# Gated attention with a routed expert layer: turned rows read back two tiles later, the router bias added once, left sums and gathers first in the attention's first step

## The chip, the cores and the metric

One core of a Trainium2 chip runs the whole program. The metric is the device time of one execution in microseconds (us). A profile is one execution recorded by the hardware profiler; its span runs from the first to the last instruction of the program. TensorE is called PE in the profile (its weight loads PEld), VectorE DVE, ScalarE ACT, GpSimd POOL and SyncE SP.

## The reference

The input x has two sequences of 1024 tokens with 512 features, in 32-bit floats.

```python
xn = layernorm(x)
# attention, one head of width 512
qkv = einsum('bsh,oh->bso', xn, w_qkv) + b_qkv
q, k, v = split(qkv, 3)
s = softmax(q @ k.T / sqrt(512)) @ v @ w_out.T + b_out
# expert layer: 8 experts, top 2
logits = xn @ router_w + router_b
topk_vals, topk_idx = top_k(logits, 2)
w = softmax(topk_vals)
h = silu(xn @ expert_w[e] + expert_b[e])      # for each expert e
combined = sum of w * h over a token's two experts
y = xn + combined @ proj_w + proj_b
g = silu(norm_w * y / sqrt(mean(y * y) + 1e-6))
out = x + s * g
```

## The kernel before, in words

The 2048 tokens are 16 tiles of 128 rows. Every engine runs its instructions in the order in which the program writes them down; semaphores keep them apart where one needs another's result. Almost all transfers are issued by SP on one queue; the stores of the experts' results (`ho_d`) are issued by ACT, the gathers by POOL. A tile of 128 x 512 floats is 256 KB.

**The loop over the tiles** (24 to 91 us). The weights of values and output are multiplied beforehand into `rwvo`, which also holds the router's columns. For tile t, `value_side(t)` multiplies the turned rows `xnT` by `rwvo` into two PSUM banks `pv` (the big pool has two such pairs, so `pv` of tile t needs what tile t - 2 held); `keep_values(t)` copies 512 columns to `vo` (ACT, L461) and the nine columns of the router and of the bias's product to `lg` (DVE, L462). In the text pv6 is the product of tile 6, vo6 and lg6 its copies.

The rows have to be normalised and turned first. `stats(g)` takes mean and variance of tiles 2g and 2g + 1 (DVE), and a square root (ACT, `std`); `shifts(g)` makes their reciprocal and shift (DVE); `rows(g)` writes the normalised rows `xn` (ACT, L333) and then issues on SP, in this order: for the tiles from 4 on a put of the rows to a scratch `xn_s` in HBM (four blocks of 128 x 128), the loads of x for tiles 8 later, the stores of the rows to `xn_d`, which the gathers read later, and again from tile 4 on the reads `xz` of the scratch (`take`). `turn_x(t)` then turns `xz` by a DVE transpose of 32 x 32 blocks (L120); tiles 0 to 3 (`DIRECT`) are turned by PE and copied by DVE (L378). Buffers: 8 of x, 5 of xn, 6 of xz, 6 of the scratch. `norm(g)` is the three together. Before the loop stand `rows(0)` and `norm(2)`; in the loop

```python
        if t == 1:
            rows(1)
            norm(3)
        if t == 3:
            turn_x(4)
            turn_x(5)
        if t % 2 == 0 and 0 < t and t + 6 < NT:
            norm(t // 2 + 3)
```

and for t from 4 on `turn_x(t + 2)` ahead of `value_side(t)`. At t = 4 SP issues four loads of the key weights `wZ`, which DVE turns at t = 8 (`turn_w`), at t = 9 and 10 DVE makes two weighted sums (`sk`, `vb`), which PE needs at t = 11 and 12.

**Routing, queries and experts** (91 to 256 us). DVE picks each token's two experts from `lg` and sorts the tokens by expert in 39 slots of 128, while PE makes the product of the query and key weights and the queries of the first sequence. Then each slot's rows are gathered (POOL), turned by way of a scratch (SP, DVE), multiplied (PE, L771), biased (DVE, L797), passed through silu (ACT, L800) and stored to `ho_d` (ACT's queue, L801).

**Attention and the rest** (256 to 541 us). Pairs of tiles go through a product of 2 x 2 blocks with seven multiplications instead of eight (Strassen's, in Winograd's form), which needs sums of blocks: `sum_left(k)` of the queries (POOL, `sw`), `sum_right` of the keys (DVE, `tw`), `sum_values` of the values (DVE, `tv`), `sum_p` of the probabilities (POOL). `scores(t)` makes the scores of tiles 0 and 1 in the plain way; `pair_scores(k)` those of a later pair, and `softmax` puts the probabilities to a scratch, which `take_p` reads back and `turn_p` turns. `fetch(t)` gathers a token's two experts' results (POOL), `scale_c` (ACT) and `combine` (DVE) add them with their weights and put them to a scratch, `take_c` and `turn_c` turn them, `project` multiplies them by `proj_w` (PE). `fetch_x` loads the rows for the sum with `proj_b`, which `add_b` makes (POOL). `queries_of(k)` makes queries of the second sequence (PE, ACT L538). `attend(k)` multiplies probabilities by values. The first step is written out at the end of the kernel, ahead of `for k in range(NP)`. Its buffers come from pool `at`, whose places are dealt out in the order in which tiles are first opened, over the room that the experts' pool `mo` has left.

Of the kernel before, what the change touches and what calls it, by code (L numbers as in the profile page):

```python
# [27 lines left out]
def kernel(  # L28
# [45 lines left out]
    def close(guard):  # L74
        guard.__exit__(None, None, None)
# [38 lines left out]
    def take(z, d):  # L114

        sp.dma_start(z.rearrange("p i f -> p (i f)"), d.rearrange("q (a i) f -> (q a) (i f)", i=4))
# [224 lines left out]
    def rows(g):  # L341

        two = (2 * g, 2 * g + 1)
        for t in two:
            xn_[t] = ln.tile([P, H], FP, tag="xn", name=f"xn{t}", bufs=5)
            normed(in_turn(xn_[t]), own(x[t]), t)
        if two[0] >= DIRECT:
            for t in two:
                xs[t] = dram.tile([4, P, P], FP, tag="xn_s", name=f"xn_s{t}", bufs=6)
                put(xs[t], xn_[t])  # L350
        for t in two:
            if t + 8 < NT:
                load_x(t + 8)
        for t in two:
            sp.dma_start(xn_d[ts(t, P), :], xn_[t])
        if two[0] >= DIRECT:
            for t in two:
                xz[t] = ln.tile([P, 4, P], FP, tag="xz", name=f"xz{t}", bufs=6)
                take(xz[t], xs.pop(t))

    def norm(g):
        stats(g)
        shifts(g)
        rows(g)
# [3 lines left out]
    def turn_x(t):  # L368
        dst = xnT[t // ST][:, :, ts(t % ST, P)]
        if t >= DIRECT:  # L370
            turn(dst, xz.pop(t))
            return
        ps = ps_mm.tile([P, 512], FP, tag="mm", name=f"xt{t}").rearrange(
            "p (j f) -> p j f", j=KC
        )
        for j in range(KC):
            pe.transpose(ps[:, j, :], xw[t][:, ts(j, P)], ident)
        dve.tensor_copy(dst, ps)  # L378
# [79 lines left out]
    def keep_values(t):  # L458
        pv = pvs.pop(t)
        dst = vo[t // ST][:, t % ST, :].rearrange("p (n f) -> p n f", n=2)  # L460
        act.copy(dst, pv[:, :, 0:HH])  # L461
        dve.tensor_tensor(lg1[:, t, :], pv[:, 0, HH : HH + E1], rb, ALU.add)  # L462


    for t in range(NT):
        if 3 < t < NT - 2:
            turn_x(t + 2)
        value_side(t)
        if t:
            keep_values(t - 1)  # L470
        if t == 1:
            rows(1)
            norm(3)
        if t == 3:
            turn_x(4)
            turn_x(5)
        if t % 2 == 0 and 0 < t and t + 6 < NT:
            norm(t // 2 + 3)
        if t == 2:
            gps.dma_start(bo, b_out.partition_broadcast(P))  # L480
        if t == 4:
            spread(sp, wZ[1], w_qkvT[:, ts(1, H)])
        if t == 8:
            turn_w(wqkT[:, KC:], wZ[1])
        if t == 9:
            sk_ = weighted(wqkT[:, KC:], bqk[:, 0], "sk")
        if t == 10:

            vb = weighted(wo, bqkv[:, 2], "vb")
        if t == 11:  # L490
            dve.tensor_copy(u, columns(sk_, "pu"))
        if t == 12:
            pvb = ps_mm.tile([P, 512], FP, tag="mm", name="pvb")
            pe.matmul(pvb, lhsT=ones, rhs=vb, start=True, stop=True)
            dve.tensor_tensor(bo, pvb, bo, ALU.add)
            close(raw_guard)
            ew_guard, ewp = pool("ew", side="right")
            ew = ewp.tile([P, E, KC, H], FP, name="ew")
            for e in range(E):
                sp.dma_start(ew[:, e], expert_w[e].rearrange("(c p) f -> p c f", p=P))  # L500
    keep_values(NT - 1)
    close(ln_guard)
    eb_guard, ebp = pool("eb", side="right")
    eb = ebp.tile([P, E, H], FP, name="eb")
# [397 lines left out]
    def sum_right(b):  # L902
        w_ = at.tile([P, 3, KH, 512], FP, tag="tw", name=f"tw{b}", bufs=1)
        return right_sums(right(b), w_, dve, 1)
# [156 lines left out]
    def take_p(t):  # L1061
        pz[t] = at.tile([P, 4, 2 * P], FP, tag="pz", name=f"pz{t}")
        take(pz[t], ps_.pop(t))
# [98 lines left out]
    def both_of(step, k, odd_first=False):  # L1162
        if k < NP:
            for t in (2 * k + 1, 2 * k) if odd_first else (2 * k, 2 * k + 1):
                step(t)


    keys, vals = sum_right(0), sum_values(0)
    for _ in range(2):
        next(keys)  # L1170
    sum_left(1)
    both_of(fetch, 0)
    sp.dma_start(pb, proj_b.partition_broadcast(P))
    both_of(fetch_x, 0)
    both_of(add_b, 0)
    sp.dma_start(nw, norm_w.partition_broadcast(P))
    scores(0)
    next(keys)
    for _ in range(3):
        next(vals)  # L1180
    take_p(0)
    scores(1)
    close(ps_guard)
    ps_guard, ps_s = pool("ps_s", bufs=4, space=PSUM)
    tw[0] = next(keys)
    both_of(scale_c, 0)
    both_of(inverse, 0)
    both_of(combine, 0)
    tv[0] = next(vals)
    take_p(1)  # L1190
    both_of(take_c, 0)
    both_of(fetch, 1)
    queries_of(0, lambda name: ps_mm.tile([P, 512], FP, tag="mm", name=name))
    for k in range(NP):
        more = k + 1 < NP
        final = k + 2 == NP
# [123 lines left out]
```

## Time and profile before

| what | us |
|---|---|
| median of 3 runs | 543.29 |
| lowest and highest | 541.87, 545.43 |
| the profiled execution's own time | 542.69 |
| its span | 541.0 |
| PE busy | 527.2 |
| DVE busy | 314.9 |
| POOL busy | 217.7 |
| ACT busy | 156.9 |

A line of a group or of the timeline names the engine, the line of the kernel, the operation and "out<-in" by the program's names, buffer numbers left out; idle time before it stands in brackets with what ended it. An instruction of PE on 32-bit floats shows as two records, so a product of four matmuls is eight records. The chain that ended last is followed back from the last instruction, at each step to what released it.

### The profile page before, as it was taken

How to read it: one execution, taken by the hardware profiler on the slowest of the kernel's cores; microseconds unless marked ns; L12 is line 12 of the kernel's file. 1: busy time of each engine (PE TensorE's matmuls, PEld its weight loads, DVE VectorE, ACT ScalarE, POOL GpSimd, SP SyncE). 2: the span in 40 equal slices, each digit the busy share in tenths (PEclk: the TensorE clock that was granted, in tenths of full speed). 3: DMA queues.
4: the chain of work that ended last, by engine and by line, in shares of the span. 5: the costliest groups of instructions: out<-in, count | busy, mean ns of one | idle time of the engine just before them, and what ended most of it. 6: DMA issues, size and time to landing. Idle time of an engine off the chain costs nothing.

```text
span 541.0 us, 5784 instructions
## 1 busy us (share of the span) xinstructions
PE 527.2 (97%) x1754; PEld 320.9 (59%) x1754; DVE 314.9 (58%) x529; ACT 156.9 (29%) x259; POOL 217.7 (40%) x231
## 2 busy tenths in 40 slices
PE   8979999999999999999999999999999999999996
PEld 6867887444444444444466666756746657484486
DVE  3645763841333333334689467376697685949595
ACT  2454312111211111111331622422425234152340
POOL 5000000023353874200276545346279755465551
PEclk9998999999999999999999999999999999999999
DMA  8879939939999999995566832723624628295502
GB/s 241 223 224 329 278 127 343 406 103 318 284 306 320 344 333 314 302 279 137 176 210 217 286 123 85 285 79 109 242 78 168 241 84 291 73 332 173 207 27 79
DMA packets 90928, 118.66 MB, mean 219 GB/s; under 512 B 6928, under 2 KB 55184, under 8 KB 90768
## 3 DMA queue, kind: packets, MB, share of 16 engines
q1 hardware_dynamic: 79344, 89.16, 51.4%
q0 software_dynamic: 5792, 18.88, 10.9%
q10 hardware_dynamic: 5760, 10.23, 5.0%
q8 instruction: 15, 0.25, 0.2%
q14 instruction: 17, 0.14, 0.1%
HBM read 73.69 MB, written 44.56 MB: 219 GB/s over the span
## 4 chain that ended last, share of the span: by engine, by line
PE 74%; DMA 10%; DVE 8%; issue 4%; ACT 1%; POOL 1%; SPq 1%; DVEq 0%; POOLq 0%; ACTq 0%
PE ph L771 20%; PE so L1104 17%; PE pp L1033 12%; PE po L970 10%; PE pq L512 5%; PE pv L450 4%; DMA wZ<-in_L_attn_w_qkv_dram 3%; PE pqk L543 3%; DMA xn_s<-xn 2%; PE pr L531 2%; DMA ho_d<-h 2%; DVE sc L1039 1%; DVE pT L120 1%; DMA xn_d<-xn 1%; DMA wo<-in_L_attn_w_out_dram 1%
## 5 line engine op out<-in xcount | busy, mean ns | idle before, releaser
L771 PE MATMUL ph<-ew,gT 128*128 x280 | 120.3, 592 | 0.0
L745 POOL DMA_INDIRECT xg<-xn_d,tok x39 | 37.2, 955 | 164.0 <-DVE npast L690 103.4
L771 PEld LDWEIGHTS ph<-ew,gT 128*128 128x128 f32 x280 | 53.2, 190 | 67.0 <-issue 67.0
L797 DVE TENSOR_TENSOR h<-ph,eb 128x512 f32<-128x512 f32 x39 | 26.9, 690 | 85.0 <-issue 53.1
L450 PE MATMUL pv<-rwvo,xnT 128*128 128x256 f32 (+1 forms) x256 | 60.3, 393 | 4.6 <-DVE lg L462 4.3
L450 PEld LDWEIGHTS pv<-rwvo,xnT 128*128 128x128 f32 x256 | 48.8, 194 | 15.0 <-DVE lg L462 6.3
L800 ACT ACTIVATE h<-h 128x512 f32<-128x512 f32 x39 | 24.6, 631 | 100.2 <-DVE h L797 97.4
L970 PE MATMUL po<-pw,ct 128*128 128x512 f32 x112 | 49.2, 592 | 0.0
L1001 ACT ACTIVATE pr<-sc,nm 128x1024 f32<-128x1024 f32 x16 | 18.3, 1146 | 89.5 <-DVE nm L998 78.4
L1111 DVE TENSOR_TENSOR o<-so,o 128x256 f32<-128x256 f32 x49 | 20.0, 421 | 39.2 <-PE so L1104 28.5
L1149 POOL TENSOR_TENSOR o<-o,base 128x512 f32<-128x512 f32 x14 | 20.6, 1491 | 47.6 <-DVE o L1114 47.6
L1033 PE MATMUL pp<-xnT,qT 128*128 128x512 f32 x84 | 39.5, 592 | 0.0
L1104 PE MATMUL so<-vo,pT 128*128 128x256 f32 x168 | 38.5, 379 | 0.0
L932 POOL DMA_INDIRECT hg<-ho_d,posi_m x32 | 32.4, 1014 | 13.2 <-issue 7.5
L970 PEld LDWEIGHTS po<-pw,ct 128*128 128x128 f32 x112 | 21.3, 190 | 25.5 <-issue 25.1
L1104 PEld LDWEIGHTS so<-vo,pT 128*128 128x128 f32 x168 | 31.9, 190 | 7.3 <-issue 2.6
L1039 DVE TENSOR_TENSOR sc<-pp,sc 128x512 f32<-128x512 f32 x49 | 31.6, 680 | 3.3 <-PE pp L1033 3.2
L120 DVE STREAM_TRANSPOSE gT<-sz 128x512 f32<-128x512 f32 x39 | 27.3, 701 | 7.1 <-DMA sz<-xs 7.1
L531 PE MATMUL pr<-xnT,wqk 128*128 128x256 f32 x128 | 29.2, 382 | 1.9 <-DVE sc L1039 1.9
L531 PEld LDWEIGHTS pr<-xnT,wqk 128*128 128x128 f32 x128 | 24.0, 190 | 8.1 <-DVE sc L1039 4.2
L120 DVE STREAM_TRANSPOSE pT<-pz 128x1024 f32<-128x1024 f32 x14 | 28.2, 2015 | 0.0
L512 PE MATMUL pq<-xnT,wqk 128*128 128x512 f32 x64 | 28.1, 594 | 0.0
(214 smaller groups left out, 773.0 us busy)
## 6 DMA issues: line engine op xcount, KB each, us to landing
xs<-xg SPq DMA_DIRECT2D x39, 256.0 KB, 4.7
sz<-xs SPq DMA_DIRECT2D x39, 256.0 KB, 4.7
ho_d<-h ACTq DMA_DIRECT2D x39, 256.0 KB, 4.9
ew<-in_L_ffn_expert_w_dram SPq DMA_DIRECT2D x8, 1024.0 KB, 13.4
ps<-pr SPq DMA_DIRECT2D x16, 512.0 KB, 2.9
pz<-ps SPq DMA_DIRECT2D x16, 512.0 KB, 4.9
x<-_attn_hidden_states_dram SPq DMA_DIRECT2D x16, 256.0 KB, 5.5
xn_d<-xn SPq DMA_DIRECT2D x16, 256.0 KB, 4.7
```

Source lines behind the costliest of these rows:

```text
L120: dve.transpose(dst.rearrange(f"p j {order} -> p i j a", a=QP), z.rearrange("p i (j b) -> p i j b", b=QP),)
L450: pe.matmul(pv[:, n, : HH + E1 * (1 - n)], lhsT=xnT[t // ST][:, c, ts(t % ST, P)], rhs=rwvo[:, c, cols], start=(c == 0), stop=(c == KC - 1),)
L512: pe.matmul(ps[:, half, :], lhsT=wqk[:, c, ts(oc, P)], rhs=xnT[0][:, c, ts(half, 512)], start=(c == 0), stop=(c == KC - 1),)
L531: pe.matmul(ps[:, :PW], lhsT=wqk[:, c, ts(oc, P)], rhs=xnT[1][:, c, ts(k, PW)], start=(c == 0), stop=(c == KC - 1),)
L745: gps.indirect_dma_start(out=xg[s], out_offset=None, in_=xn_d, in_offset=bass.IndirectOffsetOnAxis(ap=tok[:, s : s + 1], axis=0),)
L771: pe.matmul(ph, lhsT=g_[:, c, :], rhs=ew[:, ds(r, 1), c, :].rearrange("p e f -> p (e f)"), start=(c == 0), stop=(c == KC - 1),)
L797: dve.tensor_tensor(h, ph, eb[:, ds(r, 1), :].rearrange("p e f -> p (e f)"), ALU.add)
L932: gps.indirect_dma_start(out=g_, out_offset=None, in_=ho_d, in_offset=bass.IndirectOffsetOnAxis(ap=posi_m[:, n, t : t + 1], axis=0),)
L970: pe.matmul(po, lhsT=c_[:, c, :], rhs=pw[:, c, :], start=(c == 0), stop=(c == KC - 1))
L1033: pe.matmul(ps, lhsT=l_[:, c, :], rhs=r_[:, c, :], start=(c == 0), stop=(c == KH - 1))
L1039: dve.tensor_tensor(dst, ps, other, ALU.add)
L1104: pe.matmul(ps[:, :w_], lhsT=l_[:, c, :], rhs=r_[:, c, :], start=(c == 0), stop=(c == SK - 1),)
```

## The change

In the loop over the tiles, the reads of the turned rows leave `rows` and become `reads(g)`, which is called two tiles later than before or at the same tile ahead of the next `norm`; `norm(3)` moves from tile 1 to tile 2, behind `keep_values(1)`; xn has six buffers and xz five. The nine router columns are copied by ACT without a bias, and the bias `rb` is added to all 16 tiles at once after the loop. In the attention's first step `sum_left(1)` and `fetch(0)` stand first, the loads of `proj_b`, of the rows and of `norm_w` stand behind `take_p(0)`, and `inverse`, the last sum of values and `queries_of(0)` stand ahead of `scale_c` and `combine`.

```diff
@@ rows(g)
-            xn_[t] = ln.tile([P, H], FP, tag="xn", name=f"xn{t}", bufs=5)
+            xn_[t] = ln.tile([P, H], FP, tag="xn", name=f"xn{t}", bufs=6)
...
         for t in two:
             sp.dma_start(xn_d[ts(t, P), :], xn_[t])
-        if two[0] >= DIRECT:
-            for t in two:
-                xz[t] = ln.tile([P, 4, P], FP, tag="xz", name=f"xz{t}", bufs=6)
-                take(xz[t], xs.pop(t))
+    def reads(g):
+        for t in (2 * g, 2 * g + 1):
+            xz[t] = ln.tile([P, 4, P], FP, tag="xz", name=f"xz{t}", bufs=5)
+            take(xz[t], xs.pop(t))
@@ keep_values(t)
-        dve.tensor_tensor(lg1[:, t, :], pv[:, 0, HH : HH + E1], rb, ALU.add)
+        act.copy(lg1[:, t, :], pv[:, 0, HH : HH + E1])
@@ the loop over the tiles
         if t == 1:
             rows(1)
+            reads(2)
+        if t == 2:
             norm(3)
         if t == 3:
             turn_x(4)
             turn_x(5)
+            reads(3)
+        if t % 2 == 0 and 2 < t and t + 4 < NT:
+            reads(t // 2 + 2)
         if t % 2 == 0 and 0 < t and t + 6 < NT:
             norm(t // 2 + 3)
...
     keep_values(NT - 1)
+    dve.tensor_tensor(lg1, lg1, rb.unsqueeze(1).to_broadcast([P, NT, E1]), ALU.add)
@@ the attention's first step
+    sum_left(1)
+    both_of(fetch, 0)
     keys, vals = sum_right(0), sum_values(0)
     for _ in range(2):
         next(keys)
-    sum_left(1)
-    both_of(fetch, 0)
-    sp.dma_start(pb, proj_b.partition_broadcast(P))
-    both_of(fetch_x, 0)
-    both_of(add_b, 0)
-    sp.dma_start(nw, norm_w.partition_broadcast(P))
     scores(0)
     next(keys)
     for _ in range(3):
         next(vals)
     take_p(0)
+    sp.dma_start(pb, proj_b.partition_broadcast(P))
+    both_of(fetch_x, 0)
+    both_of(add_b, 0)
+    sp.dma_start(nw, norm_w.partition_broadcast(P))
     scores(1)
     close(ps_guard)
     ps_guard, ps_s = pool("ps_s", bufs=4, space=PSUM)
     tw[0] = next(keys)
+    both_of(inverse, 0)
+    tv[0] = next(vals)
+    queries_of(0, lambda name: ps_mm.tile([P, 512], FP, tag="mm", name=name))
     both_of(scale_c, 0)
-    both_of(inverse, 0)
     both_of(combine, 0)
-    tv[0] = next(vals)
     take_p(1)
     both_of(take_c, 0)
     both_of(fetch, 1)
-    queries_of(0, lambda name: ps_mm.tile([P, 512], FP, tag="mm", name=name))
```

## The prediction

> **What bounds the kernel now.** I read the page first (header, busy shares, slices), then the waits of the stretch from 24 to 95 us, the timeline of the same stretch, the table by windows, the chain of work that ended last, and the timeline from 250 to 300 us. The page:
>
> ```profile
> span 541.0 us, 5784 instructions
> PE 527.2 (97%) x1754; PEld 320.9 (59%) x1754; DVE 314.9 (58%) x529; ACT 156.9 (29%) x259; POOL 217.7 (40%) x231
> PE   8979999999999999999999999999999999999996
> DMA  8879939939999999995566832723624628295502
> ```
>
> TensorE works in 97% of the span; a slice is 13.5 us, and the only digits of PE below 9 after the start are in the third slice (27 to 40.6 us), inside the loop over the 16 tiles, and the last. There the DMA engines are full too. An edit that touches no matmul can win only the holes of PE. The waits from 24 to 95 us (engine, line, whom it waited for: us in total, times, longest):
>
> ```profile
> PE pv L450 <- DVE lg L462: 4.3, 3, 3.4
> ACT xn L333 <- DMA xn_d<-xn: 3.5, 2, 3.0
> DVE xnT L120 <- DMA xz<-xn_s: 1.7, 1, 1.7
> ```
>
> The timeline shows how they hang together (start, us, engine, line, what, idle before it and what ended that):
>
> ```profile
> 38.02 0.81 ACT L333 ACTIVATE xn<-x,shift,rstd 128x512 f32<-128x512 f32 x1 [3.05 <-DMA xn_d<-xn]
> 39.55 5.47 PE L450 MATMUL pv<-rwvo,xnT 128*128 128x256 f32 x16 [3.40 <-DVE lg L462]
> 45.26 7.45 PE L450 MATMUL pv<-rwvo,xnT 128*128 128x256 f32 x32 [0.23 <-DVE xnT L120]
> 47.75 1.10 DVE L120 STREAM_TRANSPOSE xnT<-xz 128x512 f32<-128x512 f32 x1 [1.70 <-DMA xz<-xn_s]
> 53.47 14.33 PE L450 MATMUL pv<-rwvo,xnT 128*128 128x256 f32 x64 [0.76 <-DVE lg L462]
> ```
>
> xn7 waits for a store to give its buffer back; the copy vo1 stands behind it on ACT, and pv3 has no PSUM bank until that is done. Holes of the loop: 3.40 + 0.23 + 0.76 + 0.19 (at 67.99) = 4.58 us. The second thing to see is that pv6 (53.47) hangs on a DMA: xz6 lands, DVE transposes it (47.75), then come the statistics of tiles 10 and 11, ACT's xn10 and xn11, then vo4, lg4, and PE starts: 5.72 us after the landing. By windows (us; busy and count of PE, PEld, DVE, ACT, POOL; granted clock; DMA share, GB/s) and by the chain (start, us, what):
>
> ```profile
> 36.00:44.00 8.00, 4.61 (x14) 3.59 (x14) 2.10 (x8) 3.56 (x6) 0.00 (x0) 0.79 1.01 328
> 44.00:52.00 8.00, 7.76 (x35) 6.17 (x34) 5.83 (x12) 1.66 (x4) 0.00 (x0) 1.00 1.01 355
> ...
> 32.63 5.28 DMA xn_d<-xn
> 38.97 5.57 DMA xn_s<-xn
> 44.97 4.21 DMA xn_s<-xn
> 57.56 6.75 DMA wZ<-in_L_attn_w_qkv_dram
> ```
>
> The DMA engines are full (1.01) from 36 to 52 us. SP's issues give the order, the chain the landings: the store of xn4 at 37.91, the put of tile 7 at 44.54, nine 256 KB transfers later: 0.74 us each; the put of tile 8 at 49.18, seven later: 0.66. I take 0.7 us per transfer. In the attention's first step:
>
> ```profile
> 267.58 0.72 POOL L872 TENSOR_TENSOR sw<-qT 128x256 f32<-128x256 f32 x1 [33.76 <-DMA ho_d<-h]
> 284.12 1.98 PE L1033 MATMUL pp<-tw,qT 128*128 128x512 f32 x4 [0.60 <-ACT sc L1041]
> 293.98 3.72 PE L531 MATMUL pr<-xnT,wqk 128*128 128x256 f32 x16 [0.91 <-DVE sc L1039]
> ```
>
> Holes of 1.51 us. POOL's sums start late, its gathers at 273.49 after them, ACT's scale_c waits for those and holds up queries and the copy c11 (283.47), for which PE waits.
>
> **What the Trainium skill says.** "DMA: Bandwidth & Descriptors", Queues, rings and completion order: each DMA engine takes the descriptors of a ring in ring order. The trace agrees: the landings above follow SP's order at an even pitch, 5 us after issue under load. "TensorE: Matmul & The Clock Gate", Architectural detail: ACT and DVE are strict FIFO; here vo1 does stand behind xn7. The same page, What's actually happening: after an idle window of about 3.4 us the clock drops to half until PE has been busy for such a window. Here the 3.40 us hole was followed by a mean clock of 0.79 from 36 to 44 us: (1 - 0.79) x 8 = 1.7 us of clock lost.
>
> **The change part by part.**
> *xn with 6 buffers, norm(3) after vo1.* In the new order ACT makes xn2, xn3, vo1, lg1 without a wait: vo1 at about 33.1 instead of 38.73, pv3 at 36.1. This removes the hole of 3.40. What is late next? In the built program DVE now has the copy of xnT3 (34.41, it waits for PE) ahead of the statistics of tiles 6 and 7, which move from 31.65 to 35.0; xn6 comes at 37.5 (34.15 before), so the puts of 6 and 7 start at about 38.4 and 39.1 (37.97 and 38.97 before): nothing won for the queue, which is full anyway.
> *Reads two tiles later.* SP's order of 256 KB transfers changes. xz4 and xz5 now stand behind the loads x10, x11 and the stores of xn2, xn3; xz6 and xz7 behind the puts and stores of 8 and 9; xz10 and xz11 behind the four loads of wZ. Each costs 4 places. xz4: two places after 37.91, so 39.3 before; now 39.3 + 4 x 0.7 = 42.1; with its transpose (1.09) pv4 starts at 43.2 (45.26 before). vo2 and lg2, behind xn8 and xn9, are done by 42.0, so they don't decide. pv4 and pv5 (3.51 us a tile, from the pitch of vo: 84.31, 87.82, 91.33) end at 50.2. xz6: 47.7 + 2.7 = 50.4. From there the old way of 5.72, less some 0.1 as lg no longer visits DVE: pv6 at 56.0, +2.5 against 53.47. The hole is then 5.8 us, so the half clock should follow: between 0 and 1.7 us; I take 0.9, as the window may end early. PE could start pv10 at 56.0 + 4 x 3.51 + 0.9 = 70.9.
> The other condition of pv10: vo8 and lg8 stand on ACT behind xn14 and xn15, whose statistics stand on DVE behind the transpose of xz10. The put of 10 was issued at 52.07, 4.3 after xz6's landing; now 54.7. It lands 2.3 later (shortest of this kind, nothing ahead of it), then three transfers to 59.1, then wZ. Before, the put of 11 landed at 55.30 (52.77 + 2.53), four transfers to 58.1, wZ's last at 64.31: 6.2 for wZ, or 5.7 with a pitch of 0.8. So wZ at 64.8 to 65.3, xz10 at 65.5 to 66.0, plus 5.6: pv10 at 71.1 to 71.6. I take 71.2 for both: +3.2 against 67.99. After pv10 DVE's work is ahead of PE again (sk, vb, the last transposes fit in 3.5 us a tile with the reads of 12 to 15 landed), so 3.2 stays. Bounds from the pitch of the queue: 15% faster gives +1.7, with the full clock loss +4.4.
> *Router bias once.* 16 DVE adds of 163 ns go (2.6 us, in idle time); 16 ACT copies of 9 columns come, 0.2 us each by the next rows (0.30 for std on two columns is the upper end, 0.16 from the slope of the 256 and 512 column copies, 0.37 and 0.57, the lower). ACT is 29% busy; on the path they cost what lg on DVE cost. One add of 128x144 on DVE, 0.29 us by the routing's 128x128 rows, delays the routing by some 0.25. DVE's `before` ended at 97.02 and PE took it at 98.61: hidden by product(0) and product(1); 0.25 if that cover went.
> *Attention's first step.* sum_left opened first takes the front of pool `at`: sw no longer lies on the last h buffer (its wait for ho_d until 267.4) but on gathered rows long read, so POOL's four sums run inside the expert loop. The gathers then wait for ho_d alone: 268.0 at the latest (last landing) instead of 273.49, so 5.5 us earlier. SP's loads pb, xr, nw move behind put and take of the first probabilities; add_b waits for them to about 280, the next fetch waits for combine and its put in any case. queries before scale_c: c11 no longer waits for gathers: 0.60 and 0.91 go, -1.5. sum_p and project have 10 us in hand. Bounds: 0 to -1.5, no more, since PE has no other hole here.
> Sum: +3.2 - 1.5 = +1.7. Span 541.0 becomes 542.7; the profiled execution took 542.69, 1.7 more than its span, so 544.4; the median of the runs (543.29) lies 0.6 above it: 545.0.
>
> **The rivals.**
> (A) The holes close: the reads land no later than now, so all 4.58 + 1.51 go: 537.2. For it: the wait of xn7 is the first link of the chain and is truly gone, and SP no longer stands at reads. Against: the full queue. If part of it holds, up to 540.
> (B) Only the attention's part is left: the queue's pitch is shorter once its order changes, and pv6 starts where it did: 543.3 - 1.5 = 541.8. For: 0.66 was seen late in the stretch.
> (C) The loop loses 3.2 and the attention wins nothing, because combine's put or the softmax on DVE takes the place of the gathers: 546.5. For: DVE is close to full there. Against: DVE's first sum began at 284.77 only because c11 was late.
> (D) Slower by over 1%: the half clock. Of the two holes, before pv4 (3.4 us) and before pv6 (5.8 us), the second makes PE run at half for two windows: 3.4 us lost instead of 0.9, and xz6 a further 1.4 late at a pitch of 1 us, as seen before 37.91 (puts and loads in turn). It decides once pv10 starts after 74.9 (+6.9, of which 1.5 comes back). 549.0.
> That the change doesn't do what it says is no rival: the order of each engine is fixed by the written order.
>
> **How the numbers follow.** Forecast 0.50 (543.3 to 547), A 0.12, B 0.17, C 0.13, D 0.08. The range of 540.0 to 548.0 leaves out A and D, 0.20. About 1% (5.4 us) can be told from no change: faster by more needs nearly all of A (0.07), slower by more D and a little of C (0.09), within 0.84.
>
> **What would show it.** Right: ACT's wait for xn_d gone; pv3 at about 36; the transposes of xz4, xz6, xz10 waiting for DMA at about 42, 50 and 65.5; a hole before pv6 of over 4 us with a clock below 1 after it; pv10 at 71; no hole of PE from 256 to 300; POOL's sums before 256. Wrong: xz6 transposed before 48, or PE's holes in the loop under 4 us in sum.

## The result, and the profile after

| | before | changed |
|---|---|---|
| median, us (14 runs each) | 543.13 | 546.25 |
| lowest and highest | 541.64, 546.0 | 544.07, 548.98 |
| span of the profiled execution | 541.0 | 547.3 |
| first pv to first pqk (the loop) | 66.65 | 71.49 |
| first sc to first so (the attention's first step) | 48.55 | 46.43 |

The ratio is 1.005 (95%: 1.0029 to 1.0072): the changed kernel loses 3.1 us, by less than the 1% that the prediction set as its bound. A second set of 22 runs of the changed kernel gave 545.42 and 1.0044 (1.0024 to 1.0063). The profiled execution itself took 548.98, 2.7 more than the median of its kernel; it also entered the loop 3.60 us later (28.09 against 24.49), since the first weights landed later there (the last of the first key weights at 21.0 instead of 17.7), and began it at half clock. The second set's profiled execution did not (pv0 at 25.39). So times in the loop are given from the start of pv0, and that second execution stands beside the first.

The page of the changed kernel: busy times, and PE and its clock in slices of 13.7 us.

```profile
PE 530.4 (97%) x1754; PEld 324.9 (59%) x1754; DVE 310.9 (57%) x514; ACT 158.3 (29%) x275; POOL 214.9 (39%) x231
PE   8798699999999999999999999999999999999996
PEclk9988799999999999999999999999999999999999
```

PE's count is the same, 1754. In the loop there are now two slices below 9, an 8 and a 6 (41 to 68 us), where there was one 7; the 7 ahead of them (13.7 to 27.4 us) is the late start. In the clock's row a 9 stands for 0.9 and more. The clock is below that from the third slice to the fifth; an 8 in a slice of 13.7 us is a mean, so it hides shorter stretches at half. The waits from 24 to 99 us (engine, line, whom it waited for: us in total, times, longest):

```profile
DVE xnT L120 <- DMA xz<-xn_s: 15.4, 2, 7.9
PE pv L450 <- ACT lg L462: 6.5, 2, 4.2
```

The 3.5 us of xn waiting for the store to `xn_d` are gone. In their place DVE waits 15.4 us for turned rows (1.7 before) and PE 6.5 us for lg (4.3 before). The timeline shows which tiles (start, us, engine, line, what, idle before it and what ended that):

```profile
39.22 5.47 PE L450 MATMUL pv<-rwvo,xnT 128*128 128x265 f32 x24
...
46.97 8.98 PE L450 MATMUL pv<-rwvo,xnT 128*128 128x256 f32 x32 [2.28 <-ACT lg L462]
...
54.62 1.11 DVE L120 STREAM_TRANSPOSE xnT<-xz 128x512 f32<-128x512 f32 x1 [7.91 <-DMA xz<-xn_s]
...
60.14 18.06 PE L450 MATMUL pv<-rwvo,xnT 128*128 128x256 f32 x70 [4.19 <-ACT lg L462]
...
70.57 1.10 DVE L120 STREAM_TRANSPOSE xnT<-xz 128x512 f32<-128x512 f32 x1 [7.44 <-DMA xz<-xn_s]
```

pv3 (in the row of 39.22) follows pv2 without a hole: vo1 was copied at 37.26, having waited for PE alone. Then 2.28 us are lost before pv4 and 4.19 before pv6, which stands behind xz6 (54.62): 32.05 us after pv0, against 28.98 before. DVE waits 7.44 us for xz10 (70.57). Where xz6 lost its time is seen in the issues of SP: the reads (L116) of tiles 6 and 7 in the kernel before, then in the changed one, where they are merged with those of 8 and 9; L355 are the stores of tiles 8 and 9:

```profile
43.84 1.08 SPq L116 DMA_DIRECT2D xz<-xn_s  x2
```

```profile
48.10 2.07 SPq L355 DMA_DIRECT2D xn_d<-xn  x2
50.21 2.93 SPq L116 DMA_DIRECT2D xz<-xn_s  x4
```

The read leaves at 50.21, that is 22.1 us after pv0 and not 19.4, behind the puts and stores of tiles 8 and 9; from issue to transpose it takes 4.41 us against 3.91. Of the 3.3 us that xz6 is late, 2.8 are the later issue, which is its place in the order. In the second execution, which began at full clock, the same read and transpose stand at

```profile
46.16 3.20 SPq L116 DMA_DIRECT2D xz<-xn_s  x4
...
50.85 1.08 DVE L120 STREAM_TRANSPOSE xnT<-xz 128x512 f32<-128x512 f32 x1 [6.85 <-DMA xz<-xn_s]
```

There the read leaves 20.8 us after pv0 and the transpose follows 4.69 us later: xz6 is 2.2 us late, of which 1.4 are the later issue and 0.8 the longer way from issue to transpose. Back in the first execution, after the hole (columns: stretch, us, then busy and count of PE, PEld, DVE, ACT, POOL, granted clock, DMA share, GB/s):

```profile
58.30:65.10 6.80, 4.96 (x12) 3.94 (x13) 4.36 (x9) 4.16 (x9) 0.00 (x0) 0.50 0.80 215
```

PE worked 4.96 us at half clock, which is 2.5 us lost, and then went without a hole into pv10 (76.7). In the attention's first step:

```profile
273.12 1.95 POOL L938 DMA_INDIRECT hg<-ho_d,posi_m  x1 [21.72 <-DVE nm L1004]
286.66 3.60 PE L1039 MATMUL pp<-tw,sw 128*128 128x512 f32 x8
286.86 0.58 ACT L1047 COPY sc<-pp 128x512 f32<-128x512 f32 x1
```

POOL's sums are done long before (248.3 to 251.4), the gathers start at 273.12 (8.8 us after the first scores instead of 17.6), the copy `sc` of ACT follows at 286.86, and no row of PE here carries an idle time any more. The row of the gather names DVE as what ended its wait, but the trace has the last store of h landing at 272.21, and in all nine executions with the new order the first gather starts 0.9 us after that landing. That store lands early too, 7.1 to 8.9 us after the first scores and not 11.2 to 12.8: the three stores issued 0.4 to 2.8 us after the first scores land 2.0 us after their issue with the new order and 5.0 to 6.1 with the old one, where SP issues the loads of `proj_b` and of the rows beside them. No run moved these loads alone, so that they are the cause is not shown. Routing and experts (164.7 us) and all after the first so are unchanged. So +4.84 in the loop, -2.12 in the attention, +3.60 at the start in this one execution. The starts of some products in every profiled execution of the study, in us after pv0 (last column: pqk, the loop's length):

| kernel | pv1 | pv3 | pv4 | pv6 | pv10 | pqk |
|---|---|---|---|---|---|---|
| before | 3.60 | 15.07 | 20.77 | 28.98 | 43.50 | 66.65 |
| before, again | 5.29 | 14.44 | 20.12 | 27.77 | 42.66 | 65.82 |
| changed | 5.01 | 12.92 | 18.88 | 32.05 | 48.65 | 71.49 |
| changed, again | 3.60 | 11.51 | 17.84 | 30.96 | 47.99 | 70.83 |
| attention alone | 3.60 | 14.28 | 19.98 | 27.87 | 42.85 | 65.99 |
| loop alone | 3.60 | 11.51 | 18.77 | 30.69 | 48.01 | 72.63 |
| six xn alone | 3.60 | 11.90 | 17.59 | 30.78 | 44.84 | 67.85 |
| bias alone | 5.29 | 13.54 | 18.58 | 27.94 | 43.79 | 66.63 |
| reads in rows | 3.60 | 11.51 | 17.47 | 27.97 | 42.13 | 64.98 |
| clock held | 3.60 | 11.51 | 17.75 | 30.92 | 46.74 | 69.69 |
| wZ later | 3.60 | 11.51 | 17.80 | 30.98 | 46.83 | 69.67 |
| both | 5.28 | 13.19 | 19.16 | 32.38 | 46.55 | 69.39 |
| reads ahead of stores | 3.60 | 11.51 | 17.48 | 28.27 | 42.44 | 65.38 |
| copies ahead of rows | 5.28 | 13.19 | 18.51 | 27.33 | 41.39 | 71.21 |

A pv1 of over 5 is a loop that began at half clock (the changed kernel's clock was down from 27.6 to 31.0). It puts pv1 back by 1.4 to 1.7 us; later products that wait for a DMA need not be late by as much (the kernel before, again, has pv6 at 27.77 and not at 28.98).

### The profile page after: what moved, and what is told of

Same layout as the page of the kernel before. It is cut to its first block, busy times and chain, and to the rows that moved or that the text cites. A ratio compares the mean times of both kernels' runs of the same rounds, so it can differ in the third digit from the quotient of the medians.

```text
span 547.3 us, 5796 instructions
## 1 busy us (share of the span) xinstructions
PE 530.4 (97%) x1754; PEld 324.9 (59%) x1754; DVE 310.9 (57%) x514; ACT 158.3 (29%) x275; POOL 214.9 (39%) x231
## 3 DMA queue, kind: packets, MB, share of 16 engines
q0 software_dynamic: 5792, 18.88, 11.3%
## 4 chain that ended last, share of the span: by engine, by line
PE 85%; DVE 6%; DMA 3%; issue 3%; SPq 2%; ACT 1%; DVEq 0%; ACTq 0%
PE ph L777 20%; PE so L1110 17%; PE pp L1039 14%; PE po L976 10%; PE pv L450 9%; PE pq L518 5%; PE pr L537 4%; PE sc L1020 3%; PE pqk L549 3%; DMA wo<-in_L_attn_w_out_dram 1%; DMA x<-_attn_hidden_states_dram 1%; SPq L173 1%; DMA xz<-xn_s 1%; DVE sc L1045 1%; DVE pT L120 1%
## 5 line engine op out<-in xcount | busy, mean ns | idle before, releaser
L450 PE MATMUL pv<-rwvo,xnT 128*128 128x256 f32 (+1 forms) x256 | 63.3, 410 | 6.5 <-ACT lg L462 6.5
L450 PEld LDWEIGHTS pv<-rwvo,xnT 128*128 128x128 f32 x256 | 51.9, 205 | 16.8 <-ACT lg L462 7.3
L1155 POOL TENSOR_TENSOR o<-o,base 128x512 f32<-128x512 f32 x14 | 20.8, 1506 | 48.9 <-DVE o L1120 48.9
L976 PEld LDWEIGHTS po<-pw,ct 128*128 128x128 f32 x112 | 21.3, 190 | 25.5 <-issue 25.3
L120 DVE STREAM_TRANSPOSE gT<-sz 128x512 f32<-128x512 f32 x39 | 27.4, 702 | 7.3 <-DMA sz<-xs 7.3
L120 DVE STREAM_TRANSPOSE pT<-pz 128x1024 f32<-128x1024 f32 x14 | 28.1, 2009 | 0.0
L518 PE MATMUL pq<-xnT,wqk 128*128 128x512 f32 x64 | 28.1, 594 | 0.0
```

What stands on the lines that cost most here:

```text
L120: dve.transpose(dst.rearrange(f"p j {order} -> p i j a", a=QP), z.rearrange("p i (j b) -> p i j b", b=QP),)
L450: pe.matmul(pv[:, n, : HH + E1 * (1 - n)], lhsT=xnT[t // ST][:, c, ts(t % ST, P)], rhs=rwvo[:, c, cols], start=(c == 0), stop=(c == KC - 1),)
L518: pe.matmul(ps[:, half, :], lhsT=wqk[:, c, ts(oc, P)], rhs=xnT[0][:, c, ts(half, 512)], start=(c == 0), stop=(c == KC - 1),)
L976: pe.matmul(po, lhsT=c_[:, c, :], rhs=pw[:, c, :], start=(c == 0), stop=(c == KC - 1))
```

## The experiments

In each, a ratio is to the kernel before, with its 95% interval; "loop" is first pv to first pqk of the profiled execution, "step" first sc to first so.

**The attention's step alone.** The kernel before, with the whole new order of the first step and nothing else; in short:

```diff
+    sum_left(1)
+    both_of(fetch, 0)
     keys, vals = sum_right(0), sum_values(0)
...
+    queries_of(0, lambda name: ps_mm.tile([P, 512], FP, tag="mm", name=name))
     both_of(scale_c, 0)
...
-    queries_of(0, lambda name: ps_mm.tile([P, 512], FP, tag="mm", name=name))
```

> The kernel before with the attention's first step alone changed. Queue theory (the loop loses by its reads standing later in SP's queue, the attention wins on its own): the two holes of PE, 0.60 and 0.91 us, are gone, -1.5 to -2.1 us, ratio 0.996 to 0.997. Rival (the softmax sums on DVE or the puts take the gathers' place): holes of the same sum elsewhere between 256 and 300 us, 0 us.

540.80 us, ratio 0.9966 (0.995 to 0.9982); step 46.43, loop 65.99. The attention's part wins 1.8 us by itself (1.0 to 2.7).

**The loop alone.** The changed kernel with the bias and the first step as before:

```diff
-        act.copy(lg1[:, t, :], pv[:, 0, HH : HH + E1])
+        dve.tensor_tensor(lg1[:, t, :], pv[:, 0, HH : HH + E1], rb, ALU.add)
...
-    dve.tensor_tensor(lg1, lg1, rb.unsqueeze(1).to_broadcast([P, NT, E1]), ALU.add)
```

> The change of the loop alone: reads later, six buffers of xn, norm(3) moved; bias and attention as before. Queue theory: pv6 starts 2.5 to 3 us later after pv0 than before, a hole of 4 us or more before it and half clock after it; since lg still visits DVE behind its transposes, +4 to +5.5 us, no less than the loop of the whole change lost (+4.8 in the profiled run). Rival (the nine-column copies on ACT are what delays the loop): with lg on DVE again the loss is under 1 us.

548.39 us, ratio 1.0107 (1.0073 to 1.0141); loop 72.63, step 48.59 with the two holes again (0.82 and 0.80). So the loss is the loop's. Two of the signs expected did not come: pv6 is 1.7 us late and not 2.5 to 3, and the hole ahead of it is 0.75 us and not 4. PE stood still earlier instead. The timeline shows lg2 on DVE waiting 2.10 us for ACT's vo2, with the transposes of xz4 and xz5 behind it, and PE behind these, so that pv4 starts 18.77 us after pv0 (17.84 in the changed kernel's second execution) and the clock is at half from 42.2 to 49.0:

```profile
41.89 0.17 DVE L462 TENSOR_TENSOR lg<-pv,rb 128x9 f32<-128x9 f32 x1 [2.10 <-ACT vo L461]
41.97 1.99 DVE L120 STREAM_TRANSPOSE xnT<-xz 128x512 f32<-128x512 f32 x2
...
43.19 1.19 PE L450 MATMUL pv<-rwvo,xnT 128*128 128x256 f32 x2 [3.58 <-DVE xnT L120]
```

This loop is longer than the changed kernel's (71.49, and 70.83 in its second execution), but the late pv4 is not the reason: pv10 is level with the second execution again (48.01 and 47.99). The 1.8 us come after it. There is a hole before pv10, which hangs on lg8, and the clock is at half once more from 72.9 to 76.3:

```profile
72.43 7.87 PE L450 MATMUL pv<-rwvo,xnT 128*128 128x256 f32 x27 [1.97 <-DVE lg L462]
```

**Six buffers of xn alone.** In the kernel before:

```diff
-            xn_[t] = ln.tile([P, H], FP, tag="xn", name=f"xn{t}", bufs=5)
+            xn_[t] = ln.tile([P, H], FP, tag="xn", name=f"xn{t}", bufs=6)
...
-                xz[t] = ln.tile([P, 4, P], FP, tag="xz", name=f"xz{t}", bufs=6)
+                xz[t] = ln.tile([P, 4, P], FP, tag="xz", name=f"xz{t}", bufs=5)
```

> The kernel before with six buffers of xn and five of xz, nothing else. Queue theory: ACT's wait of 3.05 us for the store is gone and the hole before pv3 shrinks to under 1 us, but xz6 lands when it did, so pv6 starts within 0.3 us of where it did (29.0 us after pv0) and the time is the same, within 0.5 us. Rival (the wait for the buffer is what the loop loses by): -3 to -4 us.

543.05 us, ratio 1.0002 (0.9982 to 1.0023); loop 67.85, step 46.83. The longest hole of the kernel before is gone, and the time with it stays where it was:

```profile
47.57 1.08 DVE L120 STREAM_TRANSPOSE xnT<-xz 128x512 f32<-128x512 f32 x1 [4.71 <-DMA xz<-xn_s]
48.50 0.16 DVE L462 TENSOR_TENSOR lg<-pv,rb 128x9 f32<-128x9 f32 x1
48.74 11.51 PE L450 MATMUL pv<-rwvo,xnT 128*128 128x256 f32 x38 [2.90 <-DVE lg L462]
```

pv3 starts at 36.40 instead of 39.55, but xz6 lands where it did (transposed at 47.57; 47.75 before). What is won before pv3 is waited for at pv4 and at pv5 (48.74), whose lg3 stands on DVE behind that transpose. The clock is then at half from 47.9 to 54.7, so pv6 starts 30.78 us after pv0; within 0.3 us of 28.98 had been expected. The loop of this execution is 1.2 us longer, and its step is 1.7 shorter with the old order (the bias alone, below, tells why), so the unchanged time is not the loop's alone. xz6, which did not move, is the full queue which the prediction held against its rival A.

**The reads back in rows.** The changed kernel, but:

```diff
         for t in two:
             sp.dma_start(xn_d[ts(t, P), :], xn_[t])
+        if two[0] >= DIRECT:
+            reads(g)
...
             rows(1)
-            reads(2)
...
-            reads(3)
-        if t % 2 == 0 and 2 < t and t + 4 < NT:
-            reads(t // 2 + 2)
```

> The changed kernel with the reads back in rows, behind the stores of the same pair; norm(3) at its new place, bias and attention as changed. Queue theory: xz6 and xz10 land where they did before, pv6 29 us after pv0, the loop within 1 us of before (up to 1.7 more where the hole of some 3.5 us before pv6 is followed by half clock), the attention's part stays: -1 to -2.5 us against before, 4 to 5.5 us faster than the changed kernel. Rival (norm(3) behind the copy of xnT3 is what costs): no faster than the changed kernel, +2 to +4 us.

541.53 us, ratio 0.998 (0.9956 to 1.0003); loop 64.98, step 46.43, xz6 transposed 22.45 us after pv0 (26.5 and 25.5 in the changed kernel), pv6 27.97 after it, 1 us sooner than expected. With buffers, norm(3), bias and attention all as changed, this one edit takes the loss away: it is the reads' place in SP's queue.

**The clock held up.** The changed kernel with 32 products of a constant tile in the hole:

```diff
+        if t == 6:
+            hold(32)
         value_side(t)
```

> The changed kernel with 32 short multiplications of a constant tile put on PE ahead of value_side(6), into the hole of 4.2 us before pv6; nothing else differs. Theory (a hole of that length costs PE up to two windows at half clock): the granted clock stays full after pv6, the products of tiles 6 to 9 are done 2.5 us earlier, but pv10 then waits for lg8, which in the changed kernel came 1.1 us ahead of pv10. So the loop goes from 71.5 us to about 70.4, and the time falls by about 1 us, to 545.2. Rival (the clock is only a mark of the hole and costs nothing, or the copies on ACT set pv10): the loop stays at 71.5 or grows by what the added products run over.

544.15 us, ratio 1.0026 (1.001 to 1.0042); loop 69.69. **wZ later.** The changed kernel with

```diff
+        if t == 6:
+            spread(sp, wZ[1], w_qkvT[:, ts(1, H)])
         if t % 2 == 0 and 0 < t and t + 6 < NT:
             norm(t // 2 + 3)
...
-        if t == 4:
-            spread(sp, wZ[1], w_qkvT[:, ts(1, H)])
```

> The changed kernel with the four loads of the key weights wZ issued at tile 6, behind the reads of tiles 10 and 11, instead of at tile 4 ahead of them; PE's clock is left alone. Theory: the read of tile 10 no longer stands behind the four loads and lands some 6 us earlier, its transpose no longer waits for it, xn14, xn15, vo8 and lg8 come earlier; but PE, slowed by the half clock after pv6, is the later of the two at pv10, so the loop wins at most 0.5 us from 71.5. A wrong theory would show as a gain of over 1.5 us (the read behind wZ decided pv10 alone) or as a loss (wZ is needed early for its turn at tile 8).

544.59 us, ratio 1.0033 (1.0016 to 1.005); loop 69.67. **Both:**

> Both edits together: multiplications of a constant ahead of value_side(6) and the loads of wZ behind the reads of tiles 10 and 11. Theory: pv10 has two conditions within about 1 us, PE's products at half clock and the late read of tile 10; each edit alone wins 1.1 or 0.5 us, both together about 2.5: the loop goes from 71.5 to about 69.0, the time to 543.7. Rival (the two effects are independent): the sum of what the two single edits gave.

543.08 us, ratio 1.0003 (0.9987 to 1.0019); loop 69.39. **The changed kernel again:**

> The changed kernel once more, nothing altered: its first profiled execution took 2.7 us more than its median, began its loop 3.6 us later than the kernel before because the first weights landed later, and had xz6 transposed 26.5 us after pv0, where the kernels with the clock held or with wZ later had 25.4 in executions that began on time. Theory (the late start is an accident of that execution and also pushed the reads back): pv0 at 24 to 25 us, xz6 transposed about 25.4 to 25.9 after pv0, pv6 about 31 after it, a loop of 69.5 to 70.5 us instead of 71.5. Rival (the change itself delays the start, or the loop of 71.5 is its normal one): pv0 again at 27 or later, or a loop of 71 to 72 after an early start.

545.42 us, ratio 1.0044 (1.0024 to 1.0063); loop 70.83 (69.5 to 70.5 expected), pv0 at 25.39, xz6 transposed 25.5 and pv6 30.96 after it: the late start, and the products at half clock behind it, were an accident of the first execution. Without them the loop loses 4.2 us against 66.65, or 5.0 against the second execution of the kernel before; the medians, 2.3 to 3.1 slower with 2.1 won in the attention, say 4.4 to 5.2. The four belong together. By the ratios the held clock wins 0.18%, wZ 0.11%, both 0.41% of 543 against the changed kernel: 1.0, 0.6 and 2.2 us, close to what was expected (1, up to 0.5, 2.5), but either alone is not clear of the noise; both together are (0.9987 to 1.0019 against 1.0024 to 1.0063). Whether both exceed the sum lies inside the intervals. The changed kernel again, then with the clock held, by windows:

```profile
55.30:62.20 6.90, 5.85 (x14) 4.60 (x15) 3.56 (x8) 3.37 (x8) 0.00 (x0) 0.51 0.95 236
```

```profile
54.00:61.00 7.00, 5.60 (x26) 4.86 (x27) 3.93 (x9) 4.32 (x11) 0.00 (x0) 1.00 0.88 225
```

In the first, 5.85 us of PE at a clock of 0.51: 2.9 us lost, and no hole afterwards. In the second PE does 26 matmul records in the time of 14, and then stands still: the timeline (of the kernel with the clock held) shows for what.

```profile
55.40 14.33 PE L450 MATMUL pv<-rwvo,xnT 128*128 128x256 f32 x64 [2.41 <-ACT lg L462]
...
65.70 1.11 DVE L120 STREAM_TRANSPOSE xnT<-xz 128x512 f32<-128x512 f32 x1 [7.31 <-DMA xz<-xn_s]
...
71.22 5.96 PE L450 MATMUL pv<-rwvo,xnT 128*128 128x256 f32 x26 [1.49 <-ACT lg L462]
```

pv10 (71.22) now has a hole of 1.49 and hangs on lg8, behind xz10, behind wZ. With wZ later that hole is absent; in that execution the half clock after the hole of 4.22 lasted one window (55.8 to 59.2), not two. That accounts for the whole gain of its loop, 1.2 us (70.83 to 69.67) where at most 0.5 was expected: 1.7 us were lost to the clock and not 2.9.

**Reads ahead of the stores.** As with the reads back in rows, and there ahead of the two stores to `xn_d`:

```diff
+        if two[0] >= DIRECT:
+            reads(g)
         for t in two:
             sp.dma_start(xn_d[ts(t, P), :], xn_[t])
```

> The changed kernel with the reads back in rows, and there ahead of the stores to xn_d instead of behind them: put, loads of x, reads, stores. Buffers, bias and attention stay as changed. Theory (the place of the reads in SP's queue decides the loop): the reads of tiles 4, 6 and so on gain two places against the kernel before, 1.3 to 1.4 us at 0.66 to 0.7 us a place; xz6 is transposed about 22 us after pv0 (23.2 in the kernel before, 22.5 with the reads in rows behind the stores), the hole before pv6 shrinks from 1.5 us to about 0.5, the loop takes about 64 us (66.7 in the kernel before, 65.0 with the reads behind the stores). With the 2.1 us of the attention's step: 540 to 541. Rival (the reads now wait for their puts at the head of SP, so that all behind them is late): xz6 no earlier, loop of 65 or more.

539.98 us, ratio 0.995 (0.993 to 0.997); loop 65.38, step 46.43. The time is as expected, the mechanism isn't: xz6 was transposed 22.76 us after pv0 (22 expected, 22.45 with the reads behind the stores), and its loop is no shorter. SP's read of tile 6 left at 42.89, 4 us ahead of its transpose, and the puts of 8 and 9, whose rows were normalised by 40.97, only behind it at 45.63:

```profile
42.89 1.06 SPq L116 DMA_DIRECT2D xz<-xn_s  x2
...
45.63 1.13 SPq L112 DMA_DIRECT2D xn_s<-xn  x2
...
46.84 1.11 DVE L120 STREAM_TRANSPOSE xnT<-xz 128x512 f32<-128x512 f32 x1 [5.54 <-DMA xz<-xn_s]
```

A read that waits for its put holds up SP and all behind it, which the rival had said. This kernel is faster than the kernel before and than the changed one; from the bias alone, which comes next, it can't be told.

**The bias alone.** In the kernel before:

```diff
-        dve.tensor_tensor(lg1[:, t, :], pv[:, 0, HH : HH + E1], rb, ALU.add)
+        act.copy(lg1[:, t, :], pv[:, 0, HH : HH + E1])
...
     keep_values(NT - 1)
+    dve.tensor_tensor(lg1, lg1, rb.unsqueeze(1).to_broadcast([P, NT, E1]), ALU.add)
```

> The kernel before with the router bias alone as changed: nine columns copied by ACT, one add after the loop. Theory: lg on ACT follows vo there, as short as the add on DVE was, so pv waits for lg 0 to 0.3 us less three times, and the one add of 0.3 us behind the loop is hidden by PE's products: 0 to -0.5 us against 543. Rival (16 more instructions on ACT, in front of the next xn, delay the chain): slower by 0.16 to 0.18 us a tile, up to +2.5 us.

539.74 us, ratio 0.9945 (0.9926 to 0.9965): 3.0 us, where 0 to 0.5 was expected. Its profiled execution is not a typical one: it took 542.69, 2.95 more than the median, and began its loop 2.0 us later than the kernel before. It has a loop of 66.63, begun at half clock (66.65 and, begun so too, 65.82 for the kernel before), so no gain is seen there, and a step of 46.61 without PE's holes, though the order of the first step is the old one. In the kernel before POOL's first sum was released by a store of h, the last but one, as its chain shows (start, us, what):

```profile
262.97 4.40 DMA ho_d<-h
...
267.58 0.73 POOL sw L872
```

The same sum in the timeline of the kernel with the bias alone, and then, with PE's hole, in that of **the kernel before once more**:

```profile
268.63 0.72 POOL L873 TENSOR_TENSOR sw<-qT 128x256 f32<-128x256 f32 x1 [32.50 <-DVE tw L886]
```

```profile
268.75 0.72 POOL L872 TENSOR_TENSOR sw<-qT 128x256 f32<-128x256 f32 x1 [36.16 <-DVE nm L997]
...
285.33 1.98 PE L1033 MATMUL pp<-tw,qT 128*128 128x512 f32 x4 [1.26 <-ACT sc L1041]
```

> The kernel before once more, nothing altered. Of four profiled executions with the old order of the attention's first step, two (the kernel before and the loop alone) took 48.6 us from the first scores to the first attend and had PE holes of 0.6 to 0.9 us, with POOL's first sum 11.7 us after the first scores, released by the store of the last h; two (six buffers of xn alone, the bias alone) took 46.6 to 46.8 us with that sum at 10.8 to 10.9. The new order took 46.43 in every one. Theory A (the old order holds a race between the landing of that store, 1.8 or 2.6 us after its issue, and PE, decided anew in each execution): 46.6 to 46.9 comes with the kernel before too, perhaps now. Theory B (it is fixed by the kernel, by how its buffers or transfers lie): 48.5 to 48.6 again, sum at 11.7. In the loop both expect 66 to 67 us with pv0 at 24 to 27.

543.75 us in a single run; step 49.11. From the first scores the sum starts at 11.7 (before), 10.8 (bias alone), 12.4 (before again); with six buffers of xn alone it was 10.9, and the step 46.83. So the old order stands at the edge: one microsecond decides whether 2 us of holes appear. These rows name DVE, but by the landings the wait is for that store: it is issued 7.0 to 7.1 us after the first scores in all five executions with the old order, the last update of its semaphore comes at 10.58 (bias alone), 10.71 (six xn), 11.49 (loop alone), 11.51 and 12.14 (the kernel before), and the sum starts 0.2 us after it every time. That is the race of theory A, though with the last store but one. The landing varies by 0.6 us within one kernel and by 1.6 between kernels; as the kernel before lost twice in two executions, these traces can't say whether a kernel fixes the side on which it falls (B). Of the 3.0 us, 1.9 are seen in this trace's step, and are the same 2 us that the changed order wins; they are the lower end of the interval (1.9 to 4.0). For the rest no trace stands, and that the typical execution has the short step too is not shown.

**Copies ahead of the rows.** The kernel with the reads ahead of the stores, and

```diff
+        if t % 2 == 0 and 3 < t and t + 6 < NT:
+            norm(t // 2 + 3)
         if 3 < t < NT - 2:
             turn_x(t + 2)
...
         if t == 3:
+            norm(4)
             turn_x(4)
...
-        if t % 2 == 0 and 0 < t and t + 6 < NT:
-            norm(t // 2 + 3)
...
         if t == 8:
+            vb = weighted(wo, bqkv[:, 2], "vb")
+        if t == 9:
             turn_w(wqkT[:, KC:], wZ[1])
-        if t == 9:
+        if t == 10:
             sk_ = weighted(wqkT[:, KC:], bqk[:, 0], "sk")
-        if t == 10:
-            vb = weighted(wo, bqkv[:, 2], "vb")
```

> The changed kernel with the reads in rows ahead of the stores (as in the run above) and three moves of program order that leave SP's order as it was there: norm(4) goes to tile 3, behind keep_values(2); from tile 4 on norm stands ahead of turn_x, so that the statistics don't queue on DVE behind a transpose that waits for its read, and the copies vo don't queue on ACT behind the rows that wait for those statistics; vb goes to tile 8, turn_w to tile 9, sk to tile 10, so that the transpose of tile 11 doesn't queue behind the wait for wZ. Theory (each engine is strictly first in, first out, so what stands behind a waiting instruction is the cost): pv4 starts at about 40.4 instead of 41.55, pv6 as soon as xz6 is turned, 48 to 49 instead of 52.35, and pv10 to pv15 follow without a hole of over 1 us: the loop takes about 62 us instead of 65.4, the time is 536 to 538. Rival (the transfers behind are late too, each later tile then waits for its own read or for wZ): the loop stays at 64 to 65 and the time at 539 to 540.

544.13 us, ratio 1.0004 (0.9978 to 1.0031); loop 71.21. A miss. As they stand, pv6 came 27.33 us after pv0 (28.27 without the moves) and pv10 41.39 (42.44). Less the 1.7 us of a start at half clock, pv4 came 16.8 us after pv0 (16.3 expected, 17.48 without the moves), pv6 25.6 (24 to 25 expected) and pv10 39.7. So up to there the moves won between 1.0 and 2.7 us, in the direction of the theory of strict order; how much of the late start pv10 still carries is not shown. All of it and more was lost afterwards:

```profile
70.70 2.49 DVE L134 STREAM_TRANSPOSE qT<-wZ 128x512 f32<-128x512 f32 x4 [3.88 <-DMA wZ<-in_L_attn_w_qkv_dram]
...
77.66 1.85 PE L307 MATMUL pu<-ones,sk 128*128 128x1 f32 x8 [3.37 <-DVE sk L298]
79.38 6.30 PE L453 MATMUL pv<-rwvo,xnT 128*128 128x256 f32 x16
```

wZ is turned at 70.70 only, when it has landed, sk had been put a tile later still, PE waited 3.37 us for it at pu, and then ran at half clock from 77.7 to 84.5: 16 records in 6.30 us.

## Why the prediction was right, and where it missed

The direction, the size within 1% and the signs of the parts were right: 545.0 (540 to 548) against 546.25, and 545.42 the second time. That the sum came so near is in part luck: the loop lost 1.0 us more than forecast (4.2, not 3.2), the attention won 0.6 more (2.1, not 1.5), and the two misses cancel in part.

**Right by its own steps.** In us after pv0, the prediction's absolute times less 24.49, against the changed kernel's second execution: pv3 11.6 predicted, 11.51 measured; xz4 transposed at 17.6, 16.6; pv4 18.7, 17.84; xz6 transposed at 25.9, 25.46; pv6 31.5, 30.96; xz10 41.0 to 41.5, 41.23. With the clock held, pv10 was bound by lg8 as foreseen, at 46.74; predicted 46.71. In the attention the sums ran inside the experts, the gathers started once the last stores allowed, and PE's holes went. xn's wait for the store went too, and with six buffers alone it shortened neither the loop nor the time.

**Mis-sized: the half clock.** The step "between 0 and 1.7 us; I take 0.9, as the window may end early" is the one that failed: it measured 2.5 and 2.9 us, since the clock stayed down for 6.8 us in both executions, two windows (the hole itself was 4.19 and 5.85; 5.8 predicted). The Trainium skill, "TensorE: Matmul & The Clock Gate", What's actually happening, says that the window is free-running, so that the same kernel varies; the trace agrees: a hole of 5.85 and one of 4.19 us were followed by two windows, one of 4.22 in the kernel with wZ later by one, and holes of 2.29 by one (reads ahead of the stores) or none (both). Taken over all traced loops, without the two holes that have the held products in them, twelve holes of 1.9 to 2.7 us were followed by one window seven times and by none five times, and seven of 2.9 to 5.9 us by two windows five times and by one twice. It goes with when the clock fell: one window in the nine cases where that was from 0.5 us before PE went on to 1.1 us after, two in the four where it was 0.9 to 1.9 us before; the fifth case of two is in the copies ahead of the rows, where the clock fell as PE went on and PE's first work was eight records of one column. The prediction tied the drop to an idle window of about 3.4 us; in these traces it came after holes of 2.0 to 2.9 us as well.

Nor is it the traced executions alone. The mean granted clock of each execution is on record; its median is 0.996 for the kernel before (67 and 48 executions), 0.990 for the changed one (14, and again 22) and 0.997 with the clock held (22). Of some 545 us that is 2.2, 5.5 and 1.6 us lost to the clock at the most, since part of it fell into holes.

In the second execution the price took pv10 to 47.99, 1.3 over the forecast; 0.3 of it came back behind pv10, and the loop lost 4.2 where 3.2 was forecast. Rival D had this price in it (3.4 lost), but its second half, a pitch of 1 us in the queue, did not come.

**Mis-sized: the attention.** -2.12 instead of -1.5. The prediction took PE's idle time for all there was to win ("no more, since PE has no other hole here"); but the ends of matmuls are modelled in the profile, and the distance between the starts of two stages shrank by more than the holes between them. From start to start the hole of 0.60 cost 0.86 us (281.64 to 285.94 is 4.30 us, the same products of the changed kernel, 290.09 to 293.53, take 3.44) and the hole of 0.91 cost 1.25 (289.38 to 297.54 is 8.16, 296.96 to 303.87 is 6.91), 2.11 in sum. Starts are the better measure. The gathers came 8.8 us sooner and not 5.5, since the last store landed sooner too, which the prediction did not have. And the old order does not always pay the 2 us, as the bias alone showed: that the prediction's profile was one in which it did is luck.

**The bias** was costed at nothing in the loop: "on the path they cost what lg on DVE cost". The copies took 0.16 to 0.18 us. The changed loop with lg on DVE was longer (72.63 against 70.83 and 71.49, one execution), but the 1.8 us came with a window at half clock behind pv10; by the medians, less the 2.16 us of the step, the two differ by 0 to 0.8 us. In the kernel before the bias alone won 3.0 us, of which the loop shows none. What it is worth in the loop stays open.

**The rivals.** A fell with six buffers alone: the hole closed, and neither the loop nor the time became shorter. B was seen in no execution with the reads later. C fell with the attention alone.

**Open:** what makes the last store of h but one land 3.6 to 5.1 us after its issue with the old order, and whether moving the loads of `proj_b` and of the rows would do for the attention what the whole new order does; neither was tried alone.

## What to carry to other kernels

On a full queue, the place of a transfer is its time: count the places that an edit moves a read back, by the pitch of that stretch, and then ask which later instruction of each in-order engine stands behind it. A hole of PE has a second price in the clock, and it is paid in whole windows: after these traces, cost a hole of about 2 to 2.7 us at 0 or 1.7 us and one of about 3 to 6 us at 1.7 to 3.4 (2.5 and 2.9 were measured, as the first window began inside the hole), not at a mean. The attention alone won 1.8 us and the bias alone 3.0, but the reads back in rows, which have both and the other moves, won 1.6: two edits that win the same 2 us don't add up, so try each part alone before summing them.

## What the runs showed of the hardware

- After two of three holes of 4 to 6 us PE's granted clock was 0.5 for two whole windows (6.8 us each) even though PE had work in 73% and 85% of that time, after the third for one; holes as short as 2.0 us were followed by one. 32 products of a constant tile in bf16 (3.65 us) ahead of such a hole kept the clock at 1.00, also where 2.4 us of hole were left.
- SP, too, keeps its order while it waits: with the reads ahead of the stores it stood at the read of tile 6 until 42.89, and the puts of rows that were ready at 40.97 left at 45.63.
- Three stores of h in a row, of 256 KB each, landed 2.0 us after their issue in all nine executions in which SP issued no loads beside them (the two stores behind them 2.0 to 4.3), and 5.0 to 6.1 us after it in all five in which it issued three loads within 1.1 us of the first scores; in the kernel before the DMA engines were busy at 0.91 from 258 to 262 us.
- The stretch before the loop, with the same instructions in all kernels here, ended between 24.0 and 28.1 us: a difference of two profiled spans under 4 us says nothing until it is taken apart by stages.
